# Linear attention with an fp4-gated FFN: sums of K as one row broadcast through DRAM, K^T xn Wv by heads in half of the array's columns, and scales' transposes and w_down's quantization at later places

## The chip, the cores and the metric

The kernel runs on one core of a Trainium2 chip. A core has a matrix engine (TensorE, PE in the profile, with its weight loads shown as PEld), a vector engine (VectorE, DVE), a scalar engine (ScalarE, ACT), a general engine (GpSimd, POOL) and a sync engine (SP), whose queue issues most of the DMAs here. The metric is the time of one execution on the device, in microseconds (us). The comparison is of the kernel before with the changed one, both on the same inputs.

## The reference, cut to what matters

The input x is 4 sequences of 2048 tokens with 256 features, float32. It is layer-normed to xn, xn passes a linear-attention layer with a feed-forward part, and the result is multiplied by the silu of a second, gated feed-forward network whose inputs and weights are rounded to fp4 in blocks of 16:

```python
xn = _layernorm(x)
# attention, 16 heads of 64
Q, K = elu(xn @ Wq + bq) + 1, elu(xn @ Wk + bk) + 1
V  = xn @ Wv + bv
KV = einsum('bshd,bshm->bhdm', K, V)
Z  = 1 / (einsum('bshd,bhd->bsh', Q, K.sum(axis=1)) + 1e-6)
o  = einsum('bshd,bhdm,bsh->bshm', Q, KV, Z)
x1 = _layer_norm(xn + o @ Wo + bo, g1, be1)
s  = _layer_norm(x1 + gelu(x1 @ W1 + b1) @ W2 + b2, g2, be2)      # 1024 wide
# gated FFN, 704 wide; q4 = value rounded to the fp4 grid times its block's scale
# scale of 16 neighbours = max(max|.| / 6, 1e-12)
h  = silu(q4(xn) @ q4(w_gate).T) * (q4(xn) @ q4(w_up).T)
g  = silu(q4(h) @ q4(w_down).T)
out = x + s * g
```

Since K^T V = (K^T xn) Wv + (sum of K) bv, the kernel never forms V: it adds up K^T xn and the sums of K over the tokens of a sequence, and multiplies by Wv once at the end.

## The kernel before

**Tiling.** Tokens are worked in blocks of T = 256 (TB = 2 groups of 128), NB = 8 blocks to a sequence ("batch"), 32 blocks in all. The 1024 key features are worked in two halves f of 512. The queries of batch b and the keys of batch b + 1 are worked in the same block: block n of a batch takes two steps `sub` of the next batch's keys (so half f = 0 of the keys is done after the batch's blocks 0 to 3, half 1 after blocks 4 to 7). The keys of batch 0 have a stage of their own ahead of the main loop (loop over n < NB, with `product`, `elu` and `onto_xn`). Blocks 24 to 31 belong to the last batch and have no keys to work.

**The stages of a half** are in the generator `m_of_half` (L479 on); `step` runs it to its next `yield`, so that its parts stand among other work. It copies K^T xn out of PSUM (pxk to xk); makes the sums of K in two forms, as columns (pks, copied into kh for the denominators) and broadcast over all partitions (pkb, copied into ksum for the bias term); multiplies xk by Wv (pkv), of which only the blocks of a head with itself are used; adds ksum times bv into kv; and multiplies by Wo (pm, copied to m). It runs eight times: for both halves of batch 0 between the first key stage and the main loop (about 113 to 155 us), and for the other six at the end of blocks 3, 7, 11, 15, 19 and 23, with pkv in the block after, behind that block's pz.

**A block's other stages**, in the order of the matmuls: `q_of` (pq, then zq on DVE), the denominators in `sums` (pz from kh and zq in tiles of 32 columns; z; z to DRAM and back as a broadcast zb; qz multiplies zq by it), `gate_up` of the next block (pg), `down` (pd), keys (pk, pxk), `attention` (pa), `ffn_2` of the block before (py), `x1_T`, and `ffn_1` (pf).

**The fp4 scales of the next block** go the way scales_h / scales_x (a reduction into scale) - `spread_scales` (L590 on: transpose pscale on PE, copy scaleT on ACT, DMA to scale_d, eight broadcasting DMAs into qT) - `quantized_x` and `quantized_h`, which multiply qT by gridT, the DMA-transposed grid values (`grid_of_h`, `grid_of_x`, `grid_T`). pg and pd read qT. `keys_in` starts the next batch's norm of one step of keys.

**The weights** of the gated FFN are quantized at the start: w_gate and w_up in the first key stage, w_down in two parts (`quantize_down`, transposes pwd on PE).

**Order.** TensorE follows the program's order throughout. VectorE and ScalarE do so until `in_order[0] = False` just ahead of the main loop; from there on, and GpSimd and SP throughout, they are placed by the framework's planner, except where `tc.issue_after` ties one operation behind another. PSUM tiles named pks, pg, pf and the like share a pool of four buffers (`mm_tile`); x1T, kv, scaleT, zb and z have one buffer each.

Of the kernel before, what the change touches and what calls it, by code (L numbers as in the profile page):

```python
# [8 lines left out]
F32 = mybir.dt.float32  # L9
BF16 = mybir.dt.bfloat16  # L10
AF = mybir.ActivationFunctionType
ALU = mybir.AluOpType
AX = mybir.AxisListType

P = 128
# [6 lines left out]
def linear_attention_gated_by_fp4_ffn(  # L22
# [61 lines left out]
    def mm_tile(name):  # L84
        return ps.tile([P, 512], F32, tag="mm", name=name)
# [11 lines left out]
    def mm(*args, **kw):  # L97
        return tc.keep_in_program_order(nc.tensor.matmul(*args, **kw))  # L98
# [380 lines left out]
    def m_of_half(b, f, dep=None, ahead=False):  # L479


        nm = f"{b}_{f}"
        fs = slice(f * HALF, (f + 1) * HALF)
        wv = batch.tile([P, ND, HALF], F32, tag="wv", name=f"wv_{nm}", bufs=1)
        load_when(dep, wv, by_chunks(Wv)[:, :, fs])
        wo = batch.tile([P, 4, D], F32, tag="wo", name=f"wo_{nm}", bufs=1)
        load_when(dep, wo, by_chunks(Wo)[:, 4 * f : 4 * f + 4, :])
        if ahead:
            yield
        if f == 0:  # L490
            kh[b] = batch.tile([P, NH, 32], F32, tag="kh", name=f"kh_{b}")
            nc.gpsimd.memset(kh[b], 0.0)
        m = m_sb[b, f] = batch.tile([P, 4, D], F32, tag="m", name=f"m_{nm}", bufs=3)
        kacc = keys.pop((b, "acc", f))
        pxk = keys.pop((b, "pxk", f))
        xk = batch.tile([P, ND, HALF], F32, tag="xk", name=f"xk_{nm}", bufs=1)
        for d in range(ND):
            scalar.copy(xk[:, d, :], pxk[d])
        pks = mm_tile(f"pks_{nm}")
        for c in range(4):  # L500
            mm(
                pks[:, c : c + 1], kacc[:, c * P : (c + 1) * P], ones[:, 0:1],
                start=True, stop=True,
            )
        for i in range(2):
            hs = slice(i * DH, (i + 1) * DH)
            r0 = 2 * f + i
            vector.tensor_copy(kh[b][hs, 4 * f : 4 * f + 4, r0], pks[hs, :4])
        pkb = mm_tile(f"pkb_{nm}")
        mm(pkb, ones, kacc, start=True, stop=True)  # L510
        ksum = work.tile([P, 4, P], F32, tag="e", name=f"ksum_{nm}", bufs=3)
        scalar.copy(ksum, pkb.rearrange("p (c f) -> p c f", c=4))
        yield
        pkv = mm_tile(f"pkv_{nm}").rearrange("p (c f) -> p c f", c=4)
        kv = work.tile([P, 4, P], F32, tag="kv", name=f"kv_{nm}", bufs=1)
        nc.gpsimd.memset(kv, 0.0)
        for ci in range(4):
            cs = slice(ci * P, (ci + 1) * P)
            for d in range(ND):
                mm(  # L520
                    pkv[:, ci, :], wv[:, d, cs], xk[:, d, cs], start=d == 0, stop=d == ND - 1
                )
        for ci in range(4):
            for h in range(2):
                hs = slice(h * DH, (h + 1) * DH)
                c = 4 * f + ci
                vector.scalar_tensor_tensor(
                    kv[hs, ci, hs], ksum[hs, ci, hs], cols["bv"][hs, c : c + 1],
                    pkv[hs, ci, hs], ALU.mult, ALU.add,
                )  # L530
        yield
        for c2 in range(2):
            pm = mm_tile(f"pm_{nm}_{c2}").rearrange("p (c d) -> p c d", c=2)
            for ci in range(2):
                mm(
                    pm[:, ci, :], kv[:, 2 * c2 + ci, :], wo[:, 2 * c2 + ci, :],
                    start=True, stop=True,
                )
            scalar.copy(m[:, 2 * c2 : 2 * c2 + 2, :], pm)
        yield  # L540
# [221 lines left out]
        nc.gpsimd.tensor_tensor(x1, x1, rows["g1"], ALU.mult)  # L762
        nc.gpsimd.tensor_tensor(x1, x1, rows["shift"], ALU.add)

    def ffn_1(n):
        x1T = blk[n].pop("x1T")
        hT = work.tile([P, NF, T], F32, tag="big", name=f"hT_{n}")
        blk[n]["hT"] = hT
        for cc in range(0, NF, 2):
            pf = mm_tile(f"pf_{n}_{cc}").rearrange("p (c t) -> p c t", c=2)  # L770
            for ci in range(2):
                c = cc + ci
                for d in range(ND):
                    mm(
                        pf[:, ci, :], w1_sb[:, d, c * P : (c + 1) * P], x1T[:, d, :],
                        start=d == 0, stop=d == ND - 1,
                    )
            for ci in range(2):
                c = cc + ci
                scalar.activation(  # L780
                    hT[:, c, :], pf[:, ci, :], AF.Gelu, bias=cols["b1"][:, c : c + 1]
                )
# [42 lines left out]
    for n in range(NB):  # L825
        more = n + 1 < NB
        tiles = [(f, j) for f in range(2) for j in range(TB)]
        k, kk = {}, {}

        def product(i):  # L830
            k[i] = key_product(xnT, *tiles[i], f"0_{n}_{tiles[i][0]}")

        def elu(i):
            f, j = tiles[i]
            kk[i], _ = key_elu(0, f, *k[i], f"0_{n}_{f}_{j}", n == 0 and j == 0)

        def onto_xn(i):
            f, j = tiles[i]
            key_xk(0, f, xn, j, kk[i], n == 0 and j == 0, not more and j == TB - 1)

        product(0)
        if more:
            st = keys_stats(n + 1)
        product(1)
        elu(0)
        product(2)
        dep = kk[0]
        elu(1)
        if not more:
            quantized_x(-1)  # L850
        if more:
            xn_next = keys_norm(n + 1, *st)
        elu(2)
        onto_xn(0)
        product(3)
        if 2 * n < 2 * I // P:
            weight = quantize_gu(range(2 * n, min(2 * n + 2, 2 * I // P)))
        elif n == 7:
            weight = quantize_down(w_down_sb, 0)
        step(weight)  # L860
        for load in later.get(n, ()):
            load(dep)
        onto_xn(1)
        step(ready)
        if n < 2:
            step(constants)
        onto_xn(2)
        elu(3)
        if more:
            xnT = keys_xnT(n + 1, xn_next)  # L870
        step(weight)
        onto_xn(3)
        ready = weight
        if n == 5:
            add_b2(dep)
            w_down_sb = load_down()
        if n == 6:
            load_xn(0)
            scales_x(0)
            spread_scales(-1, False, True)  # L880
            grid_of_x(0)
            grid_T(-1, NI * TB, NCH * TB)
            m_0 = m_of_half(0, 0, dep, ahead=True)
            step(m_0)
        if more:
            xn = xn_next
    load_xn(1)
    load_xnT(0)
    step(gate, 2)
    step(m_0)  # L890
    step(gate, 2)
    step(ready)
    weight = quantize_down(w_down_sb, 1)
    step(weight)
    step(m_0)
    step(gate, 2)
    m_half = m_of_half(0, 1)
    step(m_half)
    step(weight)
    step(gate, 9)  # L900
    step(m_0)
    step(weight)
    in_order[0] = False
    for sub in range(2):
        keys_in(1, sub)
    for j in range(TB):
        scales_h(0, j)
    scales_x(1)
    spread_scales(0, True, True)
    for j in range(TB):  # L910
        grid_of_h(0, j)
    grid_of_x(1)
# [5 lines left out]
    for n in range(NBLK):  # L918
# [4 lines left out]
        for sub in subs:  # L923
            keys_T(b + 1, sub)
        if subs:
            q_of(n)
            load_xnT(n + 1)
            kk_ins = keys_k(b + 1, subs[0])
            with tc.issue_after(kk_ins):
# [10 lines left out]
        elif n < last:  # L940
            def values():
                quantized_h(n, 0)
                return quantized_x(n)

            q_of(n, values)
            quantized_h(n, 1)
            load_xnT(n + 1)
            down(n, 0)
            sums(n)
            step(m_half)  # L950
            step(gate, 9)
            step(m_half)
            down(n, 1)
        else:
            for j in range(TB):
                quantized_h(n, j)
                down(n, j)
# [12 lines left out]
                m_half = m_of_half(b + 1, subs[1] // NB)  # L970
                step(m_half)
        bn, bin_ = divmod(n + 1, NB)
        if bn + 1 < B:
            for sub in (2 * bin_, 2 * bin_ + 1):
                keys_in(bn + 1, sub)
        if n > 0:
            ffn_2(n - 1, 0, range(0 if subs else NF // 2, NF))
            ffn_2(n - 1, 1, range(NF // 2))
# [1 line left out]
        if more[0]:  # L980
            for j in range(TB):
                scales_h(n + 1, j)
            if more[1]:
                scales_x(n + 2)
        x1_T(n)
        if more[0]:
            spread_scales(n + 1, *more)
        if n > 0:
            ffn_2(n - 1, 1, range(NF // 2, NF))
        if more[0]:  # L990
            grid_of_h(n + 1, 0)
            grid_T(n + 1, 0, NI)
# [5 lines left out]
            output(n - 1)  # L998
        if n + 1 == last:
            q_of(last)  # L1000
            sums(last)
        ffn_1(n)
    for j in range(TB):
        ffn_2(last, j)
        output(last, [j])
# [34 lines left out]
```

## Time and profile before

| | us |
|---|---|
| median of 3 runs | 1953.85 (1950.38 to 1955.07) |
| profiled execution | 1953.31 |
| its span on the core | 1951.5 |
| PE busy | 1926.4 (99%) |
| PEld busy | 1396.6 (72%) |
| DVE busy | 1267.6 (65%) |
| ACT busy | 766.4 (39%) |
| POOL busy | 538.0 (28%) |

The mean granted clock of TensorE is 0.998 of full speed. In the profile, a line of the timeline is one run of like instructions: start and length in us, engine, line of the kernel, operation, output <- inputs by their names, the part of the array in use, the shape, and the number of records (a float32 matmul leaves two). Brackets give the idle time before it and what ended that. Line L98 is the helper `mm`, L101 the helper `tr` and L114 the wrapper of VectorE and ScalarE, so groups are told apart by tile names. A line of waits gives the total in us, how many there were, and the longest. A line of windows gives the stretch, its length, the busy time of PE, PEld, DVE, ACT and POOL, then the granted clock, the DMA share and GB/s. A line of DMA issues gives output <- input, queue, operation and count, KB each, and the median us from issue to landing.

### The profile page before, as it was taken

How to read it: one execution, taken by the hardware profiler on the slowest of the kernel's cores; microseconds unless marked ns; L12 is line 12 of the kernel's file. 1: busy time of each engine (PE TensorE's matmuls, PEld its weight loads, DVE VectorE, ACT ScalarE, POOL GpSimd, SP SyncE). 2: the span in 40 equal slices, each digit the busy share in tenths (PEclk: the TensorE clock that was granted, in tenths of full speed). 3: DMA queues.
4: the chain of work that ended last, by engine and by line, in shares of the span. 5: the costliest groups of instructions: out<-in, count | busy, mean ns of one | idle time of the engine just before them, and what ended most of it. 6: DMA issues, size and time to landing. Idle time of an engine off the chain costs nothing.

```text
span 1951.5 us, 22560 instructions
## 1 busy us (share of the span) xinstructions
PE 1926.4 (99%) x8044; PEld 1396.6 (72%) x8044; DVE 1267.6 (65%) x2284; ACT 766.4 (39%) x1340; POOL 538.0 (28%) x455
## 2 busy tenths in 40 slices
PE   9989999999999999999999999999999999999998
PEld 4446677677777677777677776777776778777877
DVE  6877566666566666656665576665566666777763
ACT  2334443334443344442344433444433443334442
POOL 4431232322232232323222332222232212223221
PEclk9999999999999999999999999999999999999999
DMA  4425445354434344443443443453433444444551
GB/s 148 147 88 116 97 91 109 79 106 90 87 66 87 98 95 103 112 85 89 94 89 71 91 103 89 85 115 78 105 80 78 75 75 81 84 85 82 91 83 42
DMA packets 199785, 179.12 MB, mean 92 GB/s; under 512 B 79964, under 2 KB 161400, under 8 KB 199672
## 3 DMA queue, kind: packets, MB, share of 16 engines
q1 hardware_dynamic: 198840, 176.10, 42.4%
q10 hardware_dynamic: 832, 1.57, 0.3%
q8 instruction: 64, 1.05, 0.2%
q14 instruction: 49, 0.40, 0.1%
HBM read 129.32 MB, written 31.52 MB: 82 GB/s over the span
## 4 chain that ended last, share of the span: by engine, by line
PE 94%; DVE 3%; ACT 1%; DMA 1%; issue 0%; POOL 0%; POOLq 0%; SPq 0%; ACTq 0%; DVEq 0%
PE pg L98 15%; PE pf L98 11%; PE pa L98 11%; PE pq L98 11%; PE pk L98 11%; PE pxk L98 11%; PE py L98 10%; PE pd L98 8%; PE pz L98 2%; PE pkv L98 1%; PE pt_k L101 1%; PE pm L98 1%; PE pt_x L101 1%; DVE scale L114 1%; DVE x L114 0%
## 5 line engine op out<-in xcount | busy, mean ns | idle before, releaser
L98 PE MATMUL pg<-wgu,qT 128*128 128x352 f32 x1024 | 309.3, 460 | 0.0
L98 PEld LDWEIGHTS pg<-wgu,qT 128*128 128x128 f32 x1024 | 193.5, 190 | 116.9 <-issue 12.5
L448 POOL TENSOR_TENSOR kacc<-kacc,kk 128x512 f32<-128x512 f32 x120 | 170.8, 1423 | 304.6 <-DVE kk L114 302.5
L98 PE MATMUL pxk<-kk,xn_k 128*128 128x512 f32 x512 | 235.3, 598 | 5.2 <-DVE kk L114 5.2
L98 PE MATMUL py<-w_sb,hT 128*128 128x256 f32 x1024 | 232.9, 379 | 0.5 <-DVE s L114 0.5
L98 PE MATMUL pk<-wk_sb,xnT_k 128*128 128x512 f32 x512 | 231.9, 596 | 1.4 <-ACT xnT_k L114 1.4
L98 PE MATMUL pf<-x1T,w_sb 128*128 128x256 f32 x1024 | 227.9, 381 | 0.0
L98 PE MATMUL pa<-m,zq 128*128 128x256 f32 x1024 | 227.4, 380 | 0.4 <-ACT g L114 0.3
L98 PE MATMUL pq<-xnT,wq_sb 128*128 128x256 f32 x1024 | 226.3, 379 | 0.0
L98 PEld LDWEIGHTS pa<-m,zq 128*128 128x128 f32 x1024 | 194.1, 190 | 38.9 <-issue 10.3
L98 PEld LDWEIGHTS py<-w_sb,hT 128*128 128x128 f32 x1024 | 192.4, 190 | 35.5 <-issue 11.0
L98 PEld LDWEIGHTS pf<-x1T,w_sb 128*128 128x128 f32 x1024 | 195.6, 191 | 27.2 <-issue 0.4
L98 PEld LDWEIGHTS pq<-xnT,wq_sb 128*128 128x128 f32 x1024 | 193.6, 190 | 25.8
L114 ACT ACT_TABLE_LOAD x122 | 156.5, 1283 | 87.5 <-DVE k L114 74.2
L667 POOL TENSOR_TENSOR o<-g,be_r 128x512 f32<-128x512 f32 x32 | 51.2, 1600 | 500.7 <-ACT g L114 477.8
L114 DVE SCALAR_TENSOR_TENSOR zq<-e,q 128x512 f32<-128x512 f32 x128 | 87.6, 689 | 135.6 <-ACT e L114 135.4
L98 PE MATMUL pd<-wd,qT 128*128 128x256 f32 x768 | 172.1, 379 | 0.0
L98 PEld LDWEIGHTS pk<-wk_sb,xnT_k 128*128 128x128 f32 x512 | 97.8, 191 | 103.8 <-issue 97.1
L98 PEld LDWEIGHTS pxk<-kk,xn_k 128*128 128x128 f32 x512 | 92.4, 190 | 110.7 <-issue 79.9
L114 ACT ACTIVATE x1T<-pt_x,bcol 128x256 f32<-128x256 f32 x64 | 32.7, 561 | 351.1 <-PE pt_x L101 351.1
L98 PEld LDWEIGHTS pd<-wd,qT 128*128 128x128 f32 x768 | 145.9, 190 | 23.7
L358 POOL TENSOR_TENSOR rstd<-rstd,neg_half 128x2 f32<-128x2 f32 (+1 forms) x97 | 73.0, 752 | 315.6 <-DVE rstd L114 271.3
(121 smaller groups left out, 2343.9 us busy)
## 6 DMA issues: line engine op xcount, KB each, us to landing
zb<-z_d SPq DMA_DIRECT2D x128, 256.0 KB, 6.1
qT<-scale_d SPq DMA_DIRECT2D x248, 128.0 KB, 5.3
x_k<-in_L_attn_src_dram SPq DMA_DIRECT2D x32, 256.0 KB, 2.9
x<-in_L_attn_src_dram SPq DMA_DIRECT2D x32, 256.0 KB, 2.7
xn_d<-xn_k SPq DMA_DIRECT2D x32, 256.0 KB, 2.0
xn<-xn_d SPq DMA_DIRECT2D x32, 256.0 KB, 2.7
xnT_d<-xnT_k SPq DMA_DIRECT2D x32, 256.0 KB, 5.2
xnT<-xnT_d SPq DMA_DIRECT2D x32, 256.0 KB, 2.7
```

The source lines that it names most:

```text
L98: return tc.keep_in_program_order(nc.tensor.matmul(*args, **kw))
L101: return tc.keep_in_program_order(nc.tensor.transpose(*args, **kw))
L114: ins = op(*args, **kw)
L358: nc.gpsimd.tensor_tensor(rstd[:, j0:j1], rstd[:, j0:j1], neg_half[:, j0:j1], ALU.pow)
L448: nc.gpsimd.tensor_tensor(kacc, kacc, kk, ALU.add)
L667: nc.gpsimd.tensor_tensor(o, g, rows["be2"], ALU.mult)
```

## The change

In `m_of_half` the sums of K are made by one matmul into one row (ones as the 1-column operand, kacc moving). ScalarE copies the row, a DMA takes it to DRAM (k_d, 2 KB), and a second DMA brings it back broadcast to all 128 partitions (ksum, 256 KB). VectorE picks each partition's own columns by multiplying with the identity (own) and reducing (kcol), from which kh is filled. own takes kv's buffer and krow x1T's. There is one `yield` more. The product with Wv is made for each head alone, 64 columns at a time, written to the partitions of that head.

In block 0 `keys_in` is called after `scales_h` and `scales_x`. In the blocks without keys of a next batch `spread_scales` stands after three quarters of the second `ffn_2` part in place of a half. In the last `q_of`, `sums` stands behind the first half of `ffn_1`. At the start, `quantize_down` of part 0 moves from the key stage to behind it, part 1 to behind the planner's start, `quantized_x(-1)` behind the last `elu`, and the scales of block 0 and of x for block 1 into the hand-written order. In the instruction order that results, pwd of part 1 stands on PE between pq and pk of block 0, and ACT copies scaleT in blocks 24 to 30 behind the product m_h.

```diff
         pks = mm_tile(f"pks_{nm}")
-        for c in range(4):
-            mm(
-                pks[:, c : c + 1], kacc[:, c * P : (c + 1) * P], ones[:, 0:1],
-                start=True, stop=True,
-            )
+        mm(pks[:1, :], ones[:, 0:1], kacc, start=True, stop=True)
+        krow = work.tile([P, HALF], F32, tag="x1T", name=f"krow_{nm}", bufs=1)[:1, :]
+        scalar.copy(krow, pks[:1, :])
+        k_d = dram.tile([1, HALF], F32, tag="k_d", name=f"k_d_{nm}", bufs=2)
+        nc.sync.dma_start(k_d, krow)
+        yield
+        ksum = work.tile([P, 4, P], F32, tag="ksum", name=f"ksum_{nm}", bufs=1)
+        nc.sync.dma_start(
+            ksum, k_d.rearrange("o (c f) -> o c f", c=4).to_broadcast([P, 4, P])
+        )
+
+        own = work.tile([P, 4, P], F32, tag="kv", name=f"own_{nm}", bufs=1)
+        kcol = small.tile([P, 4], F32, tag="kcol", name=f"kcol_{nm}")
+        vector.tensor_tensor(own, ksum, ident.unsqueeze(1).to_broadcast([P, 4, P]), ALU.mult)
+        vector.tensor_reduce(kcol, own, AX.X, ALU.add)
         for i in range(2):
             hs = slice(i * DH, (i + 1) * DH)
             r0 = 2 * f + i
-            vector.tensor_copy(kh[b][hs, 4 * f : 4 * f + 4, r0], pks[hs, :4])
-        pkb = mm_tile(f"pkb_{nm}")
-        mm(pkb, ones, kacc, start=True, stop=True)
-        ksum = work.tile([P, 4, P], F32, tag="e", name=f"ksum_{nm}", bufs=3)
-        scalar.copy(ksum, pkb.rearrange("p (c f) -> p c f", c=4))
+            vector.tensor_copy(kh[b][hs, 4 * f : 4 * f + 4, r0], kcol[hs, :])
         yield
-        pkv = mm_tile(f"pkv_{nm}").rearrange("p (c f) -> p c f", c=4)
+        pkv = mm_tile(f"pkv_{nm}")[:, : 4 * DH].rearrange("p (c f) -> p c f", c=4)
...
         for ci in range(4):
-            cs = slice(ci * P, (ci + 1) * P)
             for d in range(ND):
-                mm(
-                    pkv[:, ci, :], wv[:, d, cs], xk[:, d, cs], start=d == 0, stop=d == ND - 1
-                )
+                for h in range(2):
+                    cs = slice(ci * P + h * DH, ci * P + (h + 1) * DH)
+                    mm(
+                        pkv[h * DH : (h + 1) * DH, ci, :], wv[:, d, cs], xk[:, d, cs],
+                        start=d == 0, stop=d == ND - 1,
+                    )
...
-                    pkv[hs, ci, hs], ALU.mult, ALU.add,
+                    pkv[hs, ci, :], ALU.mult, ALU.add,
...
-    def ffn_1(n):
...
+    def ffn_1(n, chunks=range(NF)):
...
-        if not more:
-            quantized_x(-1)
...
-        elif n == 7:
-            weight = quantize_down(w_down_sb, 0)
...
         elu(3)
+        if not more:
+            quantized_x(-1)
...
     load_xn(1)
     load_xnT(0)
+    down_0, down_1 = (quantize_down(w_down_sb, k) for k in range(ND))
+    step(down_0)
     step(gate, 2)
     step(m_0)
+    step(down_0)
     step(gate, 2)
-    step(ready)
-    weight = quantize_down(w_down_sb, 1)
-    step(weight)
     step(m_0)
-    step(gate, 2)
+    step(down_0)
+    scales_x(1)
+    step(gate)
+    step(m_0)
+    step(gate)
+    scales_h(0, 0)
     m_half = m_of_half(0, 1)
     step(m_half)
-    step(weight)
     step(gate, 9)
     step(m_0)
-    step(weight)
+    scales_h(0, 1)
     in_order[0] = False
+    step(down_1)
     for sub in range(2):
         keys_in(1, sub)
-    for j in range(TB):
-        scales_h(0, j)
-    scales_x(1)
     spread_scales(0, True, True)
+    step(down_1)
...
         if subs:
+            step(m_half)
             q_of(n)
+            step(down_1)
...
+            step(m_half)
             q_of(n, values)
...
-        if bn + 1 < B:
-            for sub in (2 * bin_, 2 * bin_ + 1):
-                keys_in(bn + 1, sub)
+        next_subs = (2 * bin_, 2 * bin_ + 1) if bn + 1 < B else ()
+        for sub in next_subs if n > 0 else ():
+            keys_in(bn + 1, sub)
...
                 scales_x(n + 2)
+        for sub in next_subs if n == 0 else ():
+            keys_in(bn + 1, sub)
         x1_T(n)
+
+        half_way = NF // 2 if subs else 3 * NF // 4
+        if n > 0:
+            ffn_2(n - 1, 1, range(NF // 2, half_way))
         if more[0]:
             spread_scales(n + 1, *more)
         if n > 0:
-            ffn_2(n - 1, 1, range(NF // 2, NF))
+            ffn_2(n - 1, 1, range(half_way, NF))
...
             q_of(last)
+            ffn_1(n, range(NF // 2))
             sums(last)
-        ffn_1(n)
+            ffn_1(n, range(NF // 2, NF))
+        else:
+            ffn_1(n)
```

More of the change, by code (lines that the diff above doesn't have):

```diff
@@ L763, in x1_T @@
         nc.gpsimd.tensor_tensor(x1, x1, rows["shift"], ALU.add)
-    def ffn_1(n):
[L766 to L769, printed above, removed]
+    def ffn_1(n, chunks=range(NF)):
+        x1T = blk[n]["x1T"]
+        if "hT" not in blk[n]:
+            blk[n]["hT"] = work.tile([P, NF, T], F32, tag="big", name=f"hT_{n}")
+        hT = blk[n]["hT"]
+        for cc in chunks[::2]:
             pf = mm_tile(f"pf_{n}_{cc}").rearrange("p (c t) -> p c t", c=2)
```

## The prediction

> **What bounds the kernel now.** I read the page first: shares of the engines, then the chain that ended last.
>
> ```profile
> PE 1926.4 (99%) x8044; PEld 1396.6 (72%) x8044; DVE 1267.6 (65%) x2284; ACT 766.4 (39%) x1340; POOL 538.0 (28%) x455
> ...
> PE 94%; DVE 3%; ACT 1%; DMA 1%; issue 0%; POOL 0%; POOLq 0%; SPq 0%; ACTq 0%; DVEq 0%
> ```
>
> TensorE is the bound: only 1951.5 - 1926.4 = 25 us of the span are idle. A gain must be matmul time taken out, or one of those few waits; the waits of PE say which:
>
> ```profile
> PE pscale L101 <- DVE scale L114: 8.4, 8, 4.0
> PE pxk L98 <- DVE kk L114: 5.2, 4, 2.4
> ...
> PE pz L98 <- DVE zq L114: 0.9, 1, 0.9
> PE pwd L101 <- ACT m L114: 0.6, 1, 0.6
> ```
>
> The timeline of PE gives each stage's price (start, length, records, idle before). Lengths overlap, so I take start to start.
>
> ```profile
> 153.86 0.30 PE L101 MATMUL pscale<-ident,scale 128*128 128x128 f32 x1 [1.52 <-DVE scale L114]
> ...
> 165.30 1.07 PE L98 MATMUL pz<-zq,kh 128*32 128x256 f32 x16
> 166.30 2.05 PE L98 MATMUL pkv<-xk,wv 128*128 128x128 f32 x16
> 168.19 3.60 PE L98 MATMUL pxk<-kk,xn_k 128*128 128x512 f32 x8
> ...
> 207.08 0.45 PE L101 MATMUL pscale<-ident,scale 128*128 128x128 f32 x1 [3.99 <-DVE scale L114]
> 207.32 8.59 PE L98 MATMUL pf<-x1T,w_sb 128*128 128x256 f32 x32
> ...
> 377.27 0.95 PE L98 MATMUL pks<-ones,kacc 128*128 128x1 f32 x8
> 378.08 1.10 PE L98 MATMUL pkb<-kacc,ones 128*128 128x512 f32 x2
> 379.02 5.34 PE L98 MATMUL py<-w_sb,hT 128*128 128x256 f32 x24
> ```
>
> **The change part by part.** All durations are of the one profiled execution (1953.3 us, span 1951.5, so 1.8 us outside it; the median of the runs shown, 1953.85, is 0.5 higher).
>
> *A, sums of K as one row.* Removed per half: pks 0.81 (377.27 to 378.08) and pkb 0.94 (to 379.02), 1.75 us of PE. Added: one 1x512 matmul, two records at pkb's spacing of 0.43, in a narrow-column mode. A change of mode is priced from pz: pk before it takes 3.52 from first start to pz, where pk before an ordinary matmul takes 3.43, so 0.09 per switch. New: 2 x 0.43 + 2 x 0.09 = 1.05. Saved 0.70 per half; six halves lie in the main loop: -4.2 (-5 to -4; the first two belong to the start). Beside it each half gets an ACT copy of 1x512 (at most the 0.59 of a 128x512 copy), DMAs k_d and ksum, and on DVE own 0.69, kcol 0.68. ACT and DVE are at 39% and 65%. Nearest rows for the DMAs:
>
> ```profile
> bk<-in_L_attn_bk_dram ACTq DMA_DIRECT2D x2, 256.0 KB, 3.9
> ...
> zb<-z_d SPq DMA_DIRECT2D x128, 256.0 KB, 6.1
> ...
> scale_d<-scaleT SPq DMA_DIRECT2D x32, 64.0 KB, 2.0
> xn<-xn_d SPq DMA_DIRECT2D x32, 256.0 KB, 2.7
> ```
>
> k_d 2.0; ksum 3.9, since bk is the same broadcast of one 2 KB row to 128 partitions (bounds 2.7 and 6.1). In a half that ends at 378, the row is in DRAM at about 381 and back at 385. DVE stands idle from 379.9 to 386.7 there, and kh and kv are wanted one block-half later. In the halves of the other kind own delays the h scales by about 1 us, against some 7 us between gridT's landing and its use. k_d leaves the x1T buffer about 2 us before x1T is written, and SP's two extra issues stand before scale_d, itself waiting for PE. All this I cost at nothing; gone is the cover if ksum takes over about 9.7 us (second rival).
>
> *B, pkv by heads.* Before: 16 records from 166.30 to 168.19, less the leaving of pz's mode 1.8 us. After: 32 records of half the moving columns, 0.055 each, alternating between two halves of the array. What the trace shows of neighbours in different columns is pz: 16 records of 256 columns in 1.00 us, four starts 7 ns apart, where in a row they would take 16 x 0.216 = 3.46. So abreast: 16 x 0.055 to 0.06 = 0.9, plus one more switch 0.09: 0.85 saved. But pg behind it waits for qT's multiply, which DVE begins after the eight kv operations (2.4 us), so about 0.65 reaches the path: six times, -3.9. The rule against it is in the Trainium skill, "TensorEngine Tiling (Array Packing)", Instruction Overhead: each matmul carries about 60 cycles, and one should not tile "from a dimension that's already small" (here 128 columns become 64); its Key Properties adds a drain for a mode change. If that floor were paid in a row, 32 x 0.055 + 0.09 = 1.85: +0.1 each, about +1 in all. The trace's 7 ns between starts speaks for abreast; that it shows it for quarters with long streams, not for halves with short ones, keeps the other end. I take -3.9 (-5.5 to +1).
>
> *C, keys_in behind the scales in block 0.* PE idles 3.99 us at 207.08 because scale stands behind the next keys' norms on DVE, and then runs slowly:
>
> ```profile
> 207.00:209.00 2.00, 1.92 (x5) 1.62 (x6) 1.39 (x4) 1.42 (x2) 0.57 (x1) 0.50 0.72 248
> ...
> 210.50:214.00 3.50, 3.50 (x18) 3.08 (x17) 1.70 (x4) 2.20 (x5) 1.38 (x1) 1.00 0.76 168
> ```
>
> The granted clock is 0.50 behind the idle time, 1.00 later: pf takes 8.4 us start to start for 32 x 0.216 = 6.9, so 1.5 are the clock's. The Trainium skill, "TensorE: Matmul & The Clock Gate", HAM oscillation, warns of idle stretches over some 3.4 us; the row agrees, and without the rule I could not say that a shorter wait keeps the clock. With scales first, they are ready at about 203.7, and pf starts at about 204.2 with x1T: -3.1 - 1.5 = -4.6 (-4.9 to -3.5). keys_in then comes about 3 us later, and its DMAs behind scale_d and qT on SP; keys_T needs them only at the end of pf, 7 us away.
>
> *D, pscale two matmul pairs later in blocks 25 to 30.* There PE waits for scale by 0.43, 0.48, 1.60, 0.47, 0.45, 0.43 (start to start less the usual spacing). Four py records, 0.86, ahead of it hide all but 0.7 of the third: -3.1. But the scales reach DRAM later: 0.86, and ACT now has m_h (0.81) in front of scaleT, some 1.28 in all, and with it one scale_d, eight qT and gridT on SP. These blocks already wait for that:
>
> ```profile
> 1621.88 0.26 ACT L114 COPY scaleT<-pscale 128x128 f32<-128x128 f32 x1
> 1622.03 0.81 ACT L114 ACTIVATE m_h<-h 128x704 bf16<-128x704 f32 x1
> ...
> 1634.26 1.59 DVE L114 TENSOR_TENSOR qT<-qT,gridT 128x768 f32<-128x768 f32 x2 [2.47 <-DMA qT<-scale_d]
> ...
> 1639.13 0.69 DVE L114 SCALAR_TENSOR_TENSOR zq<-e,q 128x512 f32<-128x512 f32 x1
> 1639.59 1.07 PE L98 MATMUL pz<-zq,kh 128*32 128x256 f32 x16
> ```
>
> The multiply of qT stands ahead of zq on DVE; zq ends at 1639.82, and pz's last quarter wants it at about 1640. So little slack is left, and between nothing and the whole 1.28 comes back in each block at pz or pd, 0 to 7.7 in six; I take the middle, 4.0. Net +0.9 (-3.1 to +4).
>
> *E, last block.* Its pz takes 3.4 us, waiting for zq; with half of pf between, 2.4 of that goes, but then z, its DRAM trip and qz (1.23 each) reach pa as late as before, so 2 come back: -0.4 (-2.5 to 0).
>
> *F, the stage between the first keys and block 0 (113 to 172 us).* Down_0's transposes leave the key loop, so PE comes earlier: pg at about 131.4 for 133.56. Then pwd waits for ACT and DVE behind w_down (139.0), and with DVE in written order here, own(0) stands at the head of its queue till ksum lands: krow about 137.4, k_d 139.4, ksum 143.3. Behind it are kcol, kh, the scales, eight kv (2.4), h, and own(1). Adding the operations of that queue gives pscale(0) at about 154.8, against 153.86. After it down_1's quantization (about 4 us of DVE) stands ahead of gridT(0): issue at about 167.4 for 160.47, landing 8.1 later, then qT's multiply (0.69): pg of block 1 at about 176.3, against 171.63, +4.7 (0 if the planner puts gridT first, +7 if the idle stretch also halves the clock where it counts). What A and B save in these two halves is hidden under it.
>
> **Sum.** A -4.2, B -3.9, C -4.6, D +0.9, E -0.4, F +4.7: -7.5. 1953.3 - 7.5 = 1945.8 us.
>
> **The rivals.**
> 1. *The halves do not run abreast* (floor or drain, as the skill's rule says). For: no 64-column matmul is in the trace. Against: pz. Then B is +1.0: -2.6, 1950.7 us. Chance 0.25.
> 2. *DVE stands at own* (slower side). All 128 rows of ksum come from one 2 KB row of DRAM; if that lands late, own blocks the scales and qT behind it. For: zb, a broadcast too, takes 6.1, over twice xn's 2.7 at the same size. Against: bk at 3.9. Each us over 3.9 costs one in F, and over 9.7 one in each of six halves: slower by 0.3% from 10.8 us on; at 12, -7.5 + 8.1 + 13.8 = +14.4, 1967.7 us. Chance 0.15, with the planner's other bad placements at the start in it.
> 3. *The waits vanish and give nothing back*: D -3.1, E -2.5, F 0, the rest as above: -18.3, 1935.0 us. For: only planned slack decides. Against: block 1's gridT. Chance 0.12.
>
> **How the numbers follow.** My forecast has 0.48. About 0.3%, 5.9 us, is what a measurement of this kernel can tell from no change. My forecast lies beyond it in 0.43 and within in 0.05; the first rival is within for 0.17, and 0.04 to each side; the third is faster, the second slower. Faster 0.59, same 0.22, slower 0.19. All good ends: -4.9 - 5 - 5.5 - 3.1 - 2.5 + 0 = -21, 1932; all bad ones: -3.5 - 4 + 1 + 4 + 0 + 7 = +4.5, 1958. I give 1933 to 1958, which leaves out little but the second rival.
>
> **What would show it.** After: pkv records start in pairs, about 0.95 us for 32 (right) or 1.9 (first rival); pks one row of 1.0 us in place of 1.75; no idle at pscale in block 0 and clock 1.0 in its pf; pscale of blocks 25 to 30 without idle but pz, pd or pg with new idle there, under 1 us each; pg of block 1 at about 176. Idle on PE behind DVE's own with DMA ksum as releaser, or a block 1 later than 180, would make the prediction wrong.

## The result, and the profile after

The changed kernel takes 1940.12 us (median of 6 runs, 1938.66 to 1942.96) against 1954.46 for the kernel before (6 runs, 1950.38 to 1955.98); the ratio is 0.9931, 95% interval 0.9918 to 0.9944, so about 13.5 us less (11 to 16). The forecast was 1945.8 with a range of 1933 to 1958. Profiled executions, which the parts below are measured in: span 1951.5 before, 1941.1 after, 10.4 us less. The profiled execution of the changed kernel (1942.96) is the slowest of its six.

The page of the changed kernel, shares of the engines:

```profile
PE 1918.2 (99%) x8108; PEld 1381.0 (71%) x8108; DVE 1276.6 (66%) x2300; ACT 765.2 (39%) x1340; POOL 534.9 (28%) x455
```

PE is still the bound at 99%: 8.2 us of busy time went, and 2.2 of idle time. The waits of PE say that pscale's fell and that pa has a new one:

```profile
PE pscale L101 <- DVE scale L114: 5.6, 4, 4.1
PE pxk L98 <- DVE kk L114: 3.3, 3, 1.8
PE pa L98 <- DVE zq L114: 3.0, 2, 2.8
...
PE pwd L101 <- DVE w_down L114: 0.8, 1, 0.8
PE pd L98 <- DVE qT L114: 0.5, 1, 0.5
```

The timeline of PE, changed kernel, at the places shown before (start, length, idle time before in brackets): the end of the start stage, block 0's pscale, and the sums and the product of one half.

```profile
152.03 0.33 PE L101 MATMUL pscale<-ident,scale 128*128 128x128 f32 x1 [4.11 <-DVE scale L114]
...
153.07 8.76 PE L98 MATMUL pq<-xnT,wq_sb 128*128 128x256 f32 x32
...
172.30 9.71 PE L98 MATMUL pg<-wgu,qT 128*128 128x352 f32 x32
...
204.13 0.30 PE L101 MATMUL pscale<-ident,scale 128*128 128x128 f32 x1 [0.36 <-DVE scale L114]
204.42 7.20 PE L98 MATMUL pf<-x1T,w_sb 128*128 128x256 f32 x32
211.46 1.04 PE L101 MATMUL pt_k<-ident,xn_k 128*128 128x128 f32 x8
...
373.37 1.02 PE L98 MATMUL pks<-kacc,ones 128*1 128x512 f32 x2
374.31 5.45 PE L98 MATMUL py<-w_sb,hT 128*128 128x256 f32 x24
...
400.21 1.15 PE L98 MATMUL pkv<-xk,wv 128*64 128x64 f32 x32
401.30 3.27 PE L98 MATMUL pxk<-kk,xn_k 128*128 128x512 f32 x7
```

The table below is made from the starts of pq of each block, side by side. In the two profiles of the changed kernel (here and run 1) blocks 1 to 23 agree to 0.01 us, so a part of 0.5 us can be read there in one profile. Before the main loop and from block 24 on, executions differ: the first 113 us by up to 3.5 us, each of the last blocks by up to 2.5. The two profiled executions compared here happen to agree at 113.6 (pxk behind its first long wait), so the sum can be made:

| part | forecast | profile after - before |
|---|---|---|
| F, start, up to pg of block 1 | +4.7 | +0.7 |
| C, block 0, pg of block 1 to pq of block 1 | -4.6 | -4.8 |
| A, six times | -4.2 | -0.61 each, -3.7 |
| B, six times | -3.9 | -0.55 each, -3.3 |
| D, blocks 24 to 29, without B | +0.9 | -0.3 |
| block 30 and the last (E, and what lies by chance there) | -0.4 | +0.9 |
| block 1, not forecast | 0 | +0.1 |
| sum | -7.5 | -10.4 |

### The profile page after: what moved, and what is told of

The parts are those of the page before. It is cut to its first block, busy times and chain, and to the rows that moved or that the text cites. A ratio compares the mean times of both kernels' runs of the same rounds, so it can differ in the third digit from the quotient of the medians.

```text
span 1941.1 us, 22716 instructions
## 1 busy us (share of the span) xinstructions
PE 1918.2 (99%) x8108; PEld 1381.0 (71%) x8108; DVE 1276.6 (66%) x2300; ACT 765.2 (39%) x1340; POOL 534.9 (28%) x455
## 4 chain that ended last, share of the span: by engine, by line
PE 87%; DVE 1%; DMA 1%; issue 1%; SPq 0%; POOL 0%; ACT 0%; POOLq 0%; DVEq 0%
PE pg L98 15%; PE pa L98 11%; PE pf L98 11%; PE pq L98 11%; PE py L98 11%; PE pxk L98 8%; PE pk L98 8%; PE pd L98 8%; PE pz L98 2%; PE pt_x L101 1%; PE pm L98 1%; PE pt_k L101 0%; PE pkv L98 0%; DMA zb<-z_d 0%; PE pks L98 0%
## 5 line engine op out<-in xcount | busy, mean ns | idle before, releaser
L677 POOL TENSOR_TENSOR o<-g,be_r 128x512 f32<-128x512 f32 x32 | 44.9, 1404 | 578.7 <-ACT g L114 578.7
```

What stands on the lines that cost most here:

```text
L677: nc.gpsimd.tensor_tensor(o, g, rows["be2"], ALU.mult)
```

## The experiments

Ratios are to the kernel before, with 95% intervals, and a gain in us beside a ratio is worked out from it. The experiments were run in three groups (1 to 4; 5 to 8; 9 to 12), each beside the kernel before, whose medians were 1954.42, 1952.98 and 1952.17; so medians of different groups are not compared closer than that.

**1. The changed kernel again** (no edit).

> The changed kernel once more, unaltered. Theory 1: what differed between its profiled execution (1943.0) and its median (1940.1) are waits that depend on when a DMA lands, each doubled by the clock that halves behind it: here the last block's pa should stand idle between 0 and 3 us, with the records of pa at full clock where the idle time is under about 2 us. Theory 2: the waits are the schedule's and are the same in every execution: pa idle 2.8 us and pscale of block 0 idle 4.1 us again, within 0.2. Time 1938 to 1943 by both.

Measured: 1940.09 us, ratio 0.9931 (0.9918 to 0.9943). Its profile (span 1940.9) has pscale of block 0 idle 3.9 us as before, but the last pa waits 1.59, not 2.81, and the granted clock stays at 1.00 behind that (7.4 us to the next matmul in place of 8.7); pa of blocks 29 and 30, which had waited 0.2 us at most, waits 1.60 in each. Theory 1 for the last blocks, theory 2 for the wait at the start. What that wait costs still differs: the clock stands at 0.50 for 3.41 us in both profiles, from 150.42 to 153.83 here, from the end of the idle time on, but from 153.14 to 156.55 in the first profile, 1.1 us after it. So pq takes 7.6 us here and 8.6 there (6.9 at full clock).

What the long wait was, the windows of the first profile around the last pa show (the columns are length, busy PE, PEld, DVE, ACT, POOL, then the granted clock, DMA share, GB/s):

```profile
1904.00:1906.50 2.50, 0.00 (x0) 0.00 (x0) 2.33 (x2) 0.02 (x1) 2.32 (x2) 1.00 0.28 57
1906.50:1909.00 2.50, 2.41 (x8) 2.06 (x9) 2.15 (x1) 0.00 (x0) 2.50 (x2) 0.72 0.00 0
1909.00:1911.00 2.00, 2.00 (x6) 1.53 (x6) 0.00 (x0) 0.00 (x0) 0.77 (x1) 0.50 0.00 0
```

and the tile zq on DVE there:

```profile
L114 DVE TENSOR_TENSOR zq<-zq,zb x2: 2266/2274/2282, 1904.2 to 1906.4; 128x1024 f32<-128x1024 f32 x2
```

The two qz multiplications take 2.27 us each (1.23 in the profile before, and for the first of them in run 1) while GpSimd works on o and g beside them; its first operation starts at 1904.10, 0.07 us ahead of qz. PE then stands idle 2.81 us, and the clock falls to 0.50 behind that, 1.66 us more on pa.

**2. No pairs.** Changed kernel, the same matmuls in another order:

```diff
-        for ci in range(4):
-            for d in range(ND):
-                for h in range(2):
+        for h in range(2):
+            for ci in range(4):
+                for d in range(ND):
```

> The changed kernel with the head loop outermost in the product with Wv: the same 32 records, but 16 for the left half of the columns and then 16 for the right, so no two neighbours can run abreast. If pairs gave the saving (theory 1), the stage takes 32 x 0.055 = 1.75 us in place of 0.95, and six halves lose about 0.55 to 0.8 each: +3.3 to +5 us against the changed kernel. If the saving comes from fewer columns alone and the records are anyway one behind another (theory 2), nothing changes: within 0.5 us.

Measured: 1944.03 us, ratio 0.9953 (0.9940 to 0.9967). In the timeline of its PE the stage is as long as before the change:

```profile
400.68 1.90 PE L98 MATMUL pkv<-xk,wv 128*64 128x64 f32 x32
402.51 3.70 PE L98 MATMUL pxk<-kk,xn_k 128*128 128x512 f32 x8
```

1.83 us from start to start, against 1.09 in pairs: records now start 58 ns apart, where in pairs two start 7 ns apart and the next two 58 ns on. Blocks 4, 8, 12, 16 and 20 are 0.59 longer each. So the pairs are the gain; a half as wide matmul without a partner takes 0.06 us off the stage (1.89 before the change) and nothing off the path (theory 1).

**3. Last block as before.** `sums(last)` ahead of all of `ffn_1`.

> The changed kernel with the last block's order as before: denominators ahead of all of ffn_1. In the profiled execution of the changed kernel the new order took 2.4 us out of pz but let pa idle 2.8 us behind qz and run 1.65 us longer at a lower clock. Theory 1, the new order costs: this is faster by about 1.7 us. Theory 2, the idle time at pa was of one execution: this is slower by 1 to 2.4 us. The forecast on record had the new order at -0.4, so +0.4 here.

Measured: 1941.54 us, ratio 0.9940 (0.9928 to 0.9953), overlapping the changed kernel's. In the profiles the last block alone, from its pq to the end, takes 57.7 us in all five kernels with the old order (this one, before, 5, 6 and 7). With the new order it takes 56.8 to 57.1 us in six kernels and 59.5 in three (the changed kernel, 4 and 9), the three whose last pa waits 2.81 us. So the new order gains 0.7 to 0.9 us where that wait is short, and loses 1.7 where it is long. Block 30 scatters by 2.4 us whatever the order (37.3 to 39.7), and the times don't resolve the edit.

**4. Scales' transposes at the old place.**

```diff
-        half_way = NF // 2 if subs else 3 * NF // 4
+        half_way = NF // 2
```

> The changed kernel with the scales' transposes of blocks 25 to 30 at their old place (half of the second ffn_2 part). By the forecast's step D (pscale's waits go, pd and pz wait in their place) the move is worth +0.9, so this is 0.9 us faster; by the profile of the changed kernel, whose blocks 24 to 30 sum to 1.2 us less than before beside the product's own saving, this is about 1.2 us slower. Idle at pscale of 0.4 to 1.6 us comes back in each, and pd and pz stand without idle.

Measured: 1943.99 us, ratio 0.9948 (0.9936 to 0.9961), 3.9 us above the changed kernel's median of the same group (run 1); in the profile blocks 24 to 29 take 275.7 us against 273.0 and 274.5 in the two of the changed kernel. So in this comparison the move gains, where the forecast had it cost 0.9. The reason is in the sizes of pscale's wait (start to start, less the usual spacing). Of the six, three are about 0.45 and three 1.60, where the profile before the change had one of 1.60. The same code in two blocks of this kernel, in the timeline of all engines:

```profile
1653.06 0.18 DVE L114 TENSOR_SCALAR scale<-scale 128x32 f32<-128x32 f32 x1
1653.07 1.31 POOL L772 TENSOR_TENSOR x<-x,g_r 128x512 f32<-128x512 f32 x1 [1.46 <-DVE scale L114]
...
1698.40 1.27 POOL L772 TENSOR_TENSOR x<-x,g_r 128x512 f32<-128x512 f32 x1 [1.45 <-DVE scale L114]
1698.41 1.30 DVE L114 TENSOR_SCALAR scale<-scale 128x32 f32<-128x32 f32 x1
...
1699.76 0.33 PE L101 MATMUL pscale<-ident,scale 128*128 128x128 f32 x1 [1.44 <-DVE scale L114]
```

Where VectorE's little step starts first it takes 0.18 us; where GpSimd's multiplication starts first (by 8, 71 and 103 ns in the three), the step ends with GpSimd's. The Trainium skill, "SBUF — State Buffer", Who interferes with whom, agrees: it says that a `tensor_scalar` of VectorE can need ports that it shares with GpSimd, and that the engine which issues first has them for its whole instruction while the other waits.

Three of six is one execution, though. In the profiles of kernels 5, 6 and 7, which keep the old place, the long step comes 0, 1 and 0 times in six, and with the new place it still comes 10 times in 42 (the changed kernel twice, runs 1, 2, 3, 8, 10 and 11); there it leaves pscale 0.58 us of idle time in place of 1.44. So the move hides the collision and doesn't prevent it. With B counted alike, blocks 24 to 29 take 272.4 to 275.7 us in five profiles with the old place (before, 4 to 7) and 271.7 to 274.5 in five with the new one (the changed kernel, 1, 2, 3 and 8): that the move gains against the kernel before is not shown.

**5. C alone.** Kernel before, with keys_in of block 0 behind the scales.

> The kernel before with one edit, C: in block 0 keys_in behind the scales. Theory 1 (the idle time at pscale and the slower clock behind it both go): pt_x to pf in block 0 takes 1.4 us in place of 5.0, and pf 7.0 in place of 8.4, together -5.0 us. Theory 2 (only the idle time goes, the slow records are a matter of the stage's DMA load, which is high there): -3.6. No other block changes.

Measured: 1947.17 us, ratio 0.9976 (0.9967 to 0.9985), -4.7 us. Block 0 is 4.77 shorter in the profile, as in the changed kernel. Its PE:

```profile
201.62 0.30 PE L101 MATMUL pscale<-ident,scale 128*128 128x128 f32 x1 [0.36 <-DVE scale L114]
201.91 7.20 PE L98 MATMUL pf<-x1T,w_sb 128*128 128x256 f32 x32
208.94 1.04 PE L101 MATMUL pt_k<-ident,xn_k 128*128 128x128 f32 x8
```

pf takes 7.03 us start to start, not 8.42, so the 1.4 us were the clock's (theory 1). From pg of block 1 to pq of block 1 every profile with this edit takes 40.2 us, every one without it 45.0 or 45.1.

**6. B alone.** Kernel before, with the product by heads.

> The kernel before with one edit, B: the product with Wv by heads, in pairs of half the columns. By the forecast's working 0.65 per half in six halves, -3.9; by the profile of the changed kernel -0.55 in each of blocks 4, 8, 12, 16, 20 and 24, -3.3. Rival: without the new sums the DVE queue ahead of qT's multiply is the same as before, so all 0.8 of PE's saving is lost waiting for it and nothing is gained (within 0.5).

Measured: 1948.83 us, ratio 0.9980 (0.9971 to 0.9988), -3.9 us. Blocks 4, 8, 12, 16 and 20 gain 0.49 each in the profile (0.55 in the changed kernel). Of PE's 0.8, 0.10 goes on a longer first record of pxk behind the narrow matmuls, and 0.2 is lost at pg, which starts when qT's multiply behind kv has ended, as forecast; the rival falls.

**7. A alone.** Kernel before, with the row sums, and no further `yield`.

> The kernel before with one edit, A: the sums of K as one row, by way of DRAM, with no further yield, so that own stands where the sums' copies stood. By the profile of the changed kernel -0.61 in each of blocks 3, 7, 11, 15, 19 and 23, -3.7, in the main loop. At the start the order of before puts own ahead of the scales with the DMAs' trip of 4.4 us in DVE's queue: +0 to +5 there by the forecast's step F. Sum -4 to +1. If the trip were not hidden in the main loop either (the forecast's second rival), pg or pz behind a half would stand idle and the sum is above +3.

Measured: 1958.78 us, ratio 1.0033 (1.0022 to 1.0045): **slower** by 6.4 us. In the main loop it gains the same 0.61 in each of blocks 3, 7, 11, 15, 19 and 23. At the start, VectorE, in written order there, stands for ksum with nothing put before it (first fence: DVE; second: PE):

```profile
136.15 0.52 DVE L114 TENSOR_TENSOR h<-h,pg 128x352 f32<-128x352 f32 x1 [0.50 <-PE pg L98]
141.81 0.69 DVE L114 TENSOR_TENSOR own<-ksum,ident 128x512 f32<-128x512 f32 x1 [5.13 <-DMA ksum<-k_d]
```

```profile
148.96 4.19 PE L98 MATMUL pg<-wgu,qT 128*128 128x352 f32 x8 [3.24 <-ACT h L114]
...
159.92 1.51 PE L101 MATMUL pwd<-ident,w_down 128*128 128x128 f32 x6 [5.05 <-DVE w_down L114]
```

pg and pwd wait behind it, and pq of block 1 starts 9.8 us later than before. That is the stall of the forecast's second rival, at the start only, and not by a late landing: ksum landed 3.0 us after its issue. So A needs the reordering of the start (F); what F would do without A no run shows.

**8. scales_x(1) ahead of own.** Changed kernel:

```diff
     step(gate, 2)
+    scales_x(1)
     step(m_0)
     step(down_0)
-    scales_x(1)
     step(gate)
```

> The changed kernel with scales_x(1) one step earlier in DVE's written order, ahead of own of the first half, where DVE stands idle 2.2 us for ksum. The four operations (0.69, 0.18, 0.35, 0.68) then fill that time. Theory 1: pscale of block 0 is 1.9 us earlier, PE's idle time before it is 2.2 in place of 4.1, the clock stays at 1.0 in pq behind it (8.6 us from first start to pwd becomes 6.9), and the stage up to pk of block 0 is 2 to 3.6 us shorter. Theory 2: DVE is the bound of the whole stage up to pg of block 1, so what is won at pscale is waited for at pk or pg: within 0.7 us of the changed kernel.

Measured: 1937.23 us, ratio 0.9921 (0.9909 to 0.9934). Its PE:

```profile
150.21 0.33 PE L101 MATMUL pscale<-ident,scale 128*128 128x128 f32 x1 [2.22 <-DVE scale L114]
...
151.25 7.07 PE L98 MATMUL pq<-xnT,wq_sb 128*128 128x256 f32 x32
158.16 0.60 PE L101 MATMUL pwd<-ident,w_down 128*128 128x128 f32 x4
```

pscale comes 1.8 us earlier, the idle time is 1.9 less, pq runs at full clock (6.91, 8.60 before the edit), and pg of block 1 starts at 169.97, 2.3 earlier. 1.2 of the 3.5 won by pq's end was waited for at pwd and pk, so theory 1 holds with a part of theory 2. By this profile the version beats the changed kernel by 2.3 us at that place; the ratios' intervals overlap, and run 12 with the same order shows that the start does not always go so well.

**9. GpSimd behind scale.** Kernel 4, and the first multiplication of x1 waits in blocks 24 to 29 for the reciprocal behind scale:

```diff
-        nc.gpsimd.tensor_tensor(x1, x1, rows["g1"], ALU.mult)
+        behind(nc.gpsimd.tensor_tensor(x1, x1, rows["g1"], ALU.mult), last_rs[0], n)
```

> The kernel e4 (scales' transposes at their old place) with one more edit: in blocks 24 to 29 GpSimd's multiplication of x1 waits for the reciprocal behind scale. In e4's profile pscale waits 0.45 in three of six blocks and 1.60 in three: where 1.60, the 32-column step of scale on VectorE takes 1.30 us in place of 0.18, and it starts some 10 ns behind GpSimd's 1.27 us multiplication; where 0.45, it starts 5 ns ahead of it. Theory 1 (the two engines exclude each other, and which comes first is chance): all six waits are 0.45, -3.4 us in the profile against e4, -1 to -3.5 in the times. Theory 2 (the slow step has another cause, such as a write of the DMA): waits of 1.60 remain, no change within 0.5.

Measured: 1940.12 us, ratio 0.9934 (0.9920 to 0.9947), against 0.9948 for kernel 4. All six waits are 0.43 to 0.54; blocks 24 to 31 are 3.3 us shorter than kernel 4's in the profile. In the block shown last, where it had been 1.60, all engines:

```profile
1697.87 0.18 DVE L114 TENSOR_SCALAR scale<-scale 128x32 f32<-128x32 f32 x1
...
1698.11 0.33 PE L101 MATMUL pscale<-ident,scale 128*128 128x128 f32 x1 [0.28 <-DVE scale L114]
```

Theory 1. With this, the old place of the transposes is as good as the new (the changed kernel's ratio is 0.9931).

**10 and 11. A longer stand at own.** Changed kernel, own repeated 8 and 16 times in the main loop's six halves:

```diff
+        for _ in range(8 if b else 0):
+            vector.tensor_tensor(own, ksum, ident.unsqueeze(1).to_broadcast([P, 4, P]), ALU.mult)
```

> The changed kernel with own computed nine times instead of once in the six halves of the main loop: VectorE stands 8 x 0.6 to 0.69 = 5.0 to 5.5 us longer at that place, as it would if ksum landed so much later. The forecast put the cover at 5.8 us (a landing of 3.9 us may become 9.7), so by theory 1 (hidden up to about 5.8) blocks 3 to 24 take as long as in the changed kernel within 0.3 us each. Theory 2 (no cover: VectorE feeds kh, kv and qT at once): +2 to +5 us in each of the six.

> As before with seventeen times: 16 x 0.6 to 0.69 = 10 to 11 us longer. By the forecast's cover of 5.8 us each of the six halves should lose 4 to 5 us, 25 to 30 in all. If the cover is larger than the forecast had it, less; if nothing is lost, VectorE's queue has over 10 us to give there and the second rival was never near.

Measured (one run each): 1942.88 and 1973.1 us. The repeats take 0.65 to 0.69 each. With 8, blocks 4, 12 and 20 lose nothing, blocks 8 and 16 lose 0.64 each, and block 24 1.55 (of which 0.8 is within its scatter). With 16, these six lose 3.4, 6.2, 3.5, 7.2, 3.5 and 10.1, 33.9 in all. So 5.2 us more at own are hidden but for 2 to 3 us in six halves, and 10.4 us are not. By these losses the cover is some 7 us in the first halves of a batch (blocks 4, 12 and 20). In the second ones part of the loss is the clock's, 0.50 behind waits of PE of 4.43, 4.43 and 6.56 us; less the waits alone it is 4 to 6, and run 10 gives 4.6 in blocks 8 and 16. The forecast had 5.8 for both. The repeats are a rough stand-in for a late ksum: the planner puts VectorE's other operations between them, where a late landing would hold those up too.

**12. Both remedies.** Kernel 8 with GpSimd's multiplication behind scale, and its three operations on g and o behind qz in blocks 24 to 31.

> The kernel e8 (changed kernel, scales_x(1) ahead of own) with GpSimd kept away from VectorE's critical operations in the last batch: the multiplication of x1 waits for the reciprocal behind scale, and the three operations on g and o wait for qz. Theory 1 (GpSimd's operations lengthen scale and qz by 1 to 1.3 us when they start first): qz takes 1.23 us in the last block in place of 1.5 to 2.3, pa's idle time there falls from 1.6 to 2.8 us to under 1.5 and its clock stays at 1.0, pscale waits no more than 0.1: -2 to -5 us against the changed kernel beside e8's -2.9. Theory 2 (those waits are the DMAs' of zb and qT): within 1 us of e8.

Measured: 1936.72 us (1934.72 to 1941.65), ratio 0.9923 (0.9909 to 0.9938), no better than kernel 8. In its profile qz takes 1.23 in the last block, as theory 1 had it, yet pa still waits 1.51 us: without GpSimd the wait is that of zb's DMA, theory 2. This execution, the slowest of its five, also had pscale of block 0 idle for 3.09 us where kernel 8, with the same order there, had 2.22, and its clock fell behind it (pq 8.80 us), so that its start lost 3.7 us: pg of block 1 came at 173.65, later than the changed kernel's 172.30.

## Why the prediction was right, and where it was not

The forecast of 1945.8 us is 5.7 above the measured 1940.1, well within its range. By the two profiles compared above, F was forecast 4.0 us too dear and D 1.2; errors of the other sign in A (0.5), B (0.6) and the last two blocks (1.3) hid nearly half of that, which is luck.

*A and B* rest on the right mechanism. B: the pairs do run abreast (run 2), 1.09 us for 32 records against 0.95 forecast, and what reaches the path is 0.55, not 0.65. The first rival is out: the rule of the Trainium skill that it rests on ("TensorEngine Tiling (Array Packing)", Instruction Overhead) did not bite at 64 columns, as long as a partner is in the other half. A: 0.94 us from pks to py, and 0.61 saved, not 0.70. The two switches of mode cost 0.29 and not 0.18: 0.09 going in, 0.09 going out, and the first py record is 0.10 longer.

*C* was right in both terms: the wait (from pt_x to pf 1.4 us in place of 5.0, -3.6) and the clock (-1.4), shown alone in run 5; of the two together, 0.2 was lost again behind pf.

*F* is the term that was most off: +4.7 forecast, +0.7 measured (0.5 to 1.6, counted from the same pxk, in the eight profiles with this order). The lines that this rests on, of SP and VectorE in the changed kernel, then of VectorE before:

```profile
136.34 0.23 SPq L505 DMA_DIRECT2D k_d<-krow  x1
137.47 0.35 SPq L508 DMA_DIRECT2D ksum<-k_d  x1
140.74 0.69 DVE L114 TENSOR_TENSOR own<-ksum,ident 128x512 f32<-128x512 f32 x1 [2.20 <-DMA ksum<-k_d]
...
163.24 1.85 SPq L621 DMA_TRANSPOSE gridT<-grid  x1
169.04 2.33 DVE L114 SCALAR_TENSOR_TENSOR kv<-ksum,bcol,pkv 64x64 f32<-64x64 f32 x8
171.40 0.69 DVE L114 TENSOR_TENSOR qT<-qT,gridT 128x512 f32<-128x512 f32 x1
```

```profile
168.47 2.34 DVE L114 SCALAR_TENSOR_TENSOR kv<-ksum,bcol,pkv 64x64 f32<-64x64 f32 x8 [0.33 <-PE pkv L98]
170.85 0.69 DVE L114 TENSOR_TENSOR qT<-qT,gridT 128x512 f32<-128x512 f32 x1
```

Two links up to pscale were too long, and make up 2.6 of the 2.8 us by which pscale came earlier than forecast (152.03 for 154.8). krow was ready at 136.3, not 137.4. The trip through DRAM took 4.4 us, not 5.9: k_d let the next issue go 1.1 us after its own (2.0 forecast from scale_d), and ksum landed in 3.3 (3.9 from bk). Behind pscale the step that failed is the path: the forecast let gridT's issue and landing set pg of block 1. gridT was issued at 163.24 (167.4 forecast) and landed 5.8 us later, at 169.0, yet qT's multiply began only at 171.40, when the eight kv operations had ended. Before the change it was the same: gridT landed at 168.6, and the multiply stood behind kv till 170.85. So gridT had over 2 us to spare, and what counted was PE's way to pkv: pq began 1.8 us earlier than before, but its slow clock (1.7 us), down_1's pwd behind it (0.8) and a wait of pk (0.4) used that up and 1.2 more, of which 0.7 is left at pg behind the shorter pkv. The queue itself was read rightly: own did hold VectorE for 2.2 us, PE did stand 4.1 us at pscale, and the clock did halve behind it. Runs 7 and 8 show how much hangs on what is put ahead of own: 6.4 us slower overall without any, 2.3 us better at pg with one more step (in one profile; not in that of run 12).

*D* was put at +0.9 and came out at -0.3 in the profile, by two terms. What came back at pz, pd and pg was 2.8 us and not 4.0, the middle that the forecast took of 0 to 7.7: pg behind pz starts later by 0.2, 0.8, 0.3 and 1.4 us in blocks 25 to 28 and by nothing in 29 and 30. (In run 1 it was 3.2, with 1.60 us at pa in blocks 29 and 30 besides.) And the step that took pscale's waits as fixed, at 0.45 with one odd 1.60, failed: the 1.60 is a collision with GpSimd that comes or not in each block (runs 4 and 9). Kernel 4 had three in six, so against it the move is worth -3.9 by the times and -1.2 to -2.7 by the profiles of blocks 24 to 29. The profile before had met one, and against that kernel the sign stays open.

*E*: forecast -0.4. In the last block the runs show -0.7 to -0.9 or +1.7 (run 3). The step "2 come back at pa" was about right where pa waits 1.4 to 1.7 us, and too small where GpSimd lengthens qz (2.8 us of idle time and 1.7 of clock).

*The second rival*'s stall exists: run 7 has it at the start, and run 11 in the main loop. It did not decide, because F puts work ahead of own and because ksum lands in 3.3 us. The third, all waits gone for nothing, was not reached either: the start and the last block kept theirs.

The profile's 10.4 us are less than the 14.3 of the medians. The profiled execution of the changed kernel had the long form of the last pa (4.5 us with its clock) and the slow clock at pq; that the other executions had shorter forms fits runs 1 and 8, but they left no trace, so it is not shown.

## What to carry to other kernels

Price a move by its whole chain, and ask of every wait whether it has one size: two sizes in the same code can point to a race between engines that start within a tenth of a microsecond of each other. A trip through DRAM is cheap where the waiting engine has other work ahead of it and dear where its queue is in written order; count the operations that stand behind the first one that reads the result. Small matmuls in half of the columns paid here only when neighbours alternate between the halves. And of each landing ask when its reader could have begun without it: gridT's, which the forecast put on the path, had over 2 us to spare.

## What the runs showed of the hardware

- A VectorE step of 32 columns, 0.18 us alone, took 1.20 to 1.30 us when a GpSimd multiplication of 1.27 us had started 8 to 103 ns ahead of it (run 4).
- TensorE's clock was halved, for 3.41 us or twice that, behind idle times of 2.81 us (the last pa) and 3.1 to 4.1 us (pscale of block 0), and was full behind 2.22 us (run 8) and 2.38 us (the pxk at 123 us before the change). The Trainium skill, "TensorE: Matmul & The Clock Gate", HAM oscillation, warns of idle times over about 3.4 us; by these runs less is enough.
- Half-array matmuls of 64 columns start 7 ns apart in a pair, and the next pair 58 ns later; unpaired ones 58 ns apart.
